# Half group 15 with both key tiles in parts, border terms summed on TensorE, and the 3x3 mask on VectorE, in an attention and local-attention kernel

## The chip, the cores and the metric

One core of one Trainium2 chip runs the whole program. The metric is the device time of one execution in microseconds (us). It is 3201.46 us before the change, the median of three runs (3201.24 to 3201.75).

## The reference

The input is `x`, 4 images of 64x64 pixels with 256 channels, in float32. Two layers follow each other.

```python
# layer 0: attention of every pixel of an image on all 4096 pixels of the image
q, k, v = x @ Wq + bq, x @ Wk + bk, x @ Wv + bv          # 32, 32 and 256 channels
attn = softmax(einsum('bnd,bmd->bnm', q, k))
x = gamma * einsum('bnm,bmc->bnc', attn, v) + x
# layer 1: three 3x3 depthwise filters per channel, a two-layer perceptron, a 3x3 local attention
hid = gelu(w_up1 @ conv3x3(x) + b_up1)                    # 768 -> 512 channels
h = x + w_up2 @ hid + b_up2
q, k, v = split(h @ w_qkv.T + b_qkv)                      # zero-padded at the image's border
out = h + sum over 9 neighbours of softmax(q . k / 16) * v
```

## The kernel before

**Blocks.** The 4 images are 32 blocks (`slot`, 0 to 31) of 512 pixels, 8 blocks an image, and all engines' queues are written out by hand in one order. In a block the 512 queries meet the image's 4096 keys in 16 half groups of two key tiles of 128 keys each. Half group n is worked on at point n of the block (n = 2G + half). At a point TensorE makes the scores `e` of the half group two ahead (L418), then the point's jobs of layer 1, then the products `acc` of half group n (L481). ScalarE makes `p = exp(e)` (L423). VectorE's work for half group n+1 (`add_up`, `low_and_gap`) stands at the end of point n, and after it come some steps of the 3x3 filters (`perc`, L687 and L693): `share` gives their number at each point: 2, 6, 8, 4, 7, 2, 7, 4, 6, 4, 3, 1, and none at points 12 to 15.

**Whole or in parts.** A key tile is multiplied either whole, in float32 (`acc<-p,v`, one product for each of two halves of the channels), or in parts: p is split into a rounded high part (`ph` or `oh`, ScalarE), a low part (`pl` or `ol`, L446 or L510) and a gap (`pg` or `og`, L447 or L520), which make three products for each half of the channels in the quicker fp32r format. Half groups 2, 4, ..., 14 have both tiles in parts by one operation on 1024 columns. In odd half groups one tile (the second) is in parts, by operations on 512 columns. In those of `BOTH_IN_PARTS` the first is too. This holds in the 25 "full" blocks (3 to 6, 8 to 14, 16 to 22, 24 to 30). The first tile's four pieces (values loaded by SyncE, high, low, gap) lie in the one buffer `hid`, which the perceptron also uses; those of the second lie in four buffers `vs`. Both show as `vo`, `oh`, `ol`, `og` in the trace. The values' parts are written to HBM once for each image by `project_v`.

**Layer 1, three to five blocks behind.** `border_terms` runs at the end of `update` (point 7): for the two side columns (8 pixels each), and in the first and last block of an image also for a row of 2 x 32 pixels, it weights the two halves of `h`'s channels with `wc` and adds them into `edge`; `border` (point 14) sums `edge` over the partitions by a product with ones (`c<-edge,ones`, L1004) and takes the exponential into `pad`. `local_values` (points 10 and 0) makes two tiles of local values with a bias. `scores` (points 11 and 12, one half of the columns each) makes the local scores `s`, their exponential `lp` (ScalarE, L1081) and the mask by `near` (GpSimd, L1086, in blocks before 30). `local_sum` (after the second mask) adds pieces of `lp` into `lsum` on GpSimd (L1109). GpSimd's queue also issues the transfers `sent<-p` (`send`, L498 and L500), by which the DMA sums up the weights.

**The end of a block.** After half group 15, VectorE adds the weights up (`den`, L513 to L529), transposes `den` and the `lsum` of an older block (L547), reduces each (`parts`, L548), and reads out the accumulators (`evacuate`, L567), all ahead of the next block's first perceptron sum (`hid<-hid_bc`, L807). At point 0 of the next block TensorE makes `hid_a`, `hid_bc`, the local values, and then `dps<-parts,fold` (L576, in `finish`), ahead of the next half group 0. `hid_a` and the local values take one of the two banks called `m`, and `hid_bc` and `dps` take the other by turns, so that `dps` has to wait until L807 has read `hid_bc`. In the second of the lines below the banks' order is fixed.

```python
            return {0: 0, NBLK - 1: RB - 1}.get(s % NBLK)          # edge_row: which blocks have a border row
            return bank("m", name) if turns[-1] == "m" else turns[-1](name)   # job_bank
            ps = bank("m", f"dps_{s}")[:, :n]                       # finish
```

Of the kernel before, what the change touches and what calls it, by code (L numbers as in the profile page):

```python
# [9 lines left out]
F32 = mybir.dt.float32  # L10
F32R = mybir.dt.float32r
AF = mybir.ActivationFunctionType
ALU = mybir.AluOpType
AX = mybir.AxisListType
PSUM = bass.MemoryType.PSUM

P = 128
B, H, W, C = 4, 64, 64, 256
N = H * W
CQK = C // 8  # L20
CH = C // P
HP, WP = H + 2, W + 2
NB = 512
RB = NB // W
# [18 lines left out]
NSLOT = B * NBLK  # L43
# [7 lines left out]
BELOW = 1.0 - 2.0**-13  # L51
IN_PARTS = (2, 4, 6, 8, 10, 12, 14)
ONE_IN_PARTS = (1, 3, 5, 7, 9, 11, 13, 15)
BOTH_IN_PARTS = (11, 13)
BY_DMA = (3, 5, 7, 9, 11, 13)
BY_DMA_IF_FULL = tuple(range(14))

# [5 lines left out]
def attention_then_perception_kernel(  # L63
# [19 lines left out]
    nc = tc.nc  # L83
# [8 lines left out]
    ones = const.tile([P, P], F32, tag="ones", name="ones")  # L92
# [8 lines left out]
    def unshifted():  # L101
        fctx = ExitStack()
        pool = fctx.enter_context(tc.tile_pool(name="fast", bufs=1))
# [4 lines left out]
        def tile_of(shape, tag, name, bufs=1):  # L108
            return pool.tile(shape, F32, tag=tag, name=name, bufs=bufs)
# [84 lines left out]
        def watch(values):  # L194

            n = values.free_size()
            for i in range(0, n, P):
                at = watched[:, : min(P, n - i)]
                nc.gpsimd.tensor_tensor(at, at, values[:, i : min(n, i + P)], ALU.add)
# [22 lines left out]
        def full(s):  # L222
            return in_two_sums(s) and s > 1 and s % NBLK < NBLK - 1
# [4 lines left out]
        def alone(s, n):  # L228

            return [i for i, ns in enumerate((BOTH_IN_PARTS, ONE_IN_PARTS)) if full(s) and n in ns]  # L230

# [110 lines left out]
        def project_v(s, pair, tag="m"):  # L342
# [10 lines left out]
            n = 2 * (s % NBLK) + pair  # L353
            split, one, both = (n in ns for ns in (IN_PARTS, ONE_IN_PARTS, BOTH_IN_PARTS))
            h = packed_h[:, s, bass.ts(pair, 2 * C)].rearrange("p (t c) -> p t c", c=C)
# [54 lines left out]
        parts_, inverses, turneds, evacuated = {}, {}, {}, {}  # L410
# [120 lines left out]
        def squares(t):  # L531
            return t.rearrange("p (j r) -> p j r", r=SQ)
# [6 lines left out]
        def partial_sums(s):  # L539


            a = shared(s)
            parts_[s] = tile_of([P, 2, NJ], "parts", f"parts_{s}")
            turneds[s] = tile_of([P, CH, NB], "xc", f"turned_{s}", 2)
            todo = [sums[s][:, 0, :]] + ([] if a is None else [lsums.pop(a)])
            for i, t in enumerate(todo):
                nc.vector.transpose(turneds[s][:, i, :], t)  # L547
                nc.vector.tensor_reduce(  # L548
                    parts_[s][:, i, :], squares(turneds[s][:, i, :]), axis=AX.X, op=ALU.add
                )  # L550
            watch(parts_[s][:, : len(todo), :].rearrange("p i j -> p (i j)"))

        def on_all(values, turned, out, copy=nc.vector.tensor_copy):

# [82 lines left out]
        def late_tile(name):  # L637

            if not thirds:
                t = perc_tile(name).rearrange("p s n -> p (s n)")  # L640
                thirds[:] = [t[:, i * NB : (i + 1) * NB] for i in range(3)]
            return thirds.pop(0)
# [237 lines left out]
        guides, lvs, near_ws, late, results, totals = [], {}, {}, {}, {}, {}  # L880
        wg = pool.tile([P, CH, C], F32, tag="wg", name="wg")
        small = pool.tile([P, 2 * CH + 1], F32, tag="small", name="small")
        bg, wc, bc = small[:, :CH], small[:, CH : 2 * CH], small[0:1, 2 * CH :]
# [82 lines left out]
        def edge_row(s):  # L966
            return {0: 0, NBLK - 1: RB - 1}.get(s % NBLK)

        edge = pool.tile([P, 2 * RB + W], F32, tag="edge", name="edge")

        def border_parts(s):

# [15 lines left out]
        def border_terms(s):  # L988


            for to, of in border_parts(s):
                nc.scalar.mul(edge[:, to], of(0), wc[:, 0:1])
                nc.vector.scalar_tensor_tensor(
                    edge[:, to], of(1), wc[:, 1:2], edge[:, to], ALU.mult, ALU.add
                )

        def border(s):


            ps = job_bank(f"c_{s}")  # L1000
            row = edge_row(s)
            n_side = 2 * RB
            n = border_parts(s)[-1][0].stop
            nc.tensor.matmul(ps[0:1, :n], lhsT=ones[:, 0:1], rhs=edge[:, :n], start=True, stop=True)  # L1004
            one = pad[0:1, :]
            nc.scalar.activation(one[:, :n], ps[0:1, :n], AF.Exp, bias=bc, scale=-(C**-0.5))
            nc.gpsimd.tensor_scalar(one[:, :n], one[:, :n], 3.0, None, ALU.mult)
            if row is not None:

                ends = one[:, n_side : n : W - 1]  # L1010
                nc.gpsimd.tensor_scalar(ends, ends, 2.0 / 3.0, None, ALU.mult)
# [4 lines left out]
        def local_values(s, t):  # L1016
            ps = job_bank(f"lv_{s}_{t}")
            for half in range(2):
                for kin in range(CH):
                    nc.tensor.matmul(  # L1020
                        ps[:, half * C : (half + 1) * C],
                        lhsT=keys_of(s, t, half, kin), rhs=wlv[:, kin, :],
                        start=(kin == 0), stop=(kin == CH - 1),
                    )
            for half in range(2):
                if s < NSLOT - 2:
                    lvs[s, t, half] = tile_of([P, C], "lv", f"lv_{s}_{t}_{half}", 8)
                else:
                    if not half:
                        late[s, t] = late_tile(f"lv_{s}_{t}")  # L1030
                    lvs[s, t, half] = late[s, t][:, half * C : (half + 1) * C]
                lv = lvs[s, t, half]
                nc.vector.tensor_tensor(lv, ps[:, half * C : (half + 1) * C], blv, ALU.add)
                if s >= NSLOT - 1:

                    square = tile_of([P, 2, NB], "den", f"lv_{s}_{t}_{half}_2")[:, 0, :C]
                    nc.gpsimd.tensor_tensor(square, lv, lv, ALU.mult)
                    watch(square)

        def pieces(s):  # L1040

# [9 lines left out]
        def scores(s, half):  # L1051


            g = s % NBLK
            ps = job_bank(f"s_{s}_{half}")

            tiles, rows, top = (2, QR, 0) if s < NSLOT else (1, UP, RB)
            n = tiles * rows * QW
            for t in range(tiles):
                for kin in range(CH):  # L1060
                    nc.tensor.matmul(  # L1061
                        ps[:, t * QR * QW : t * QR * QW + rows * QW].rearrange(
                            "p (h w) -> p h w", w=QW
                        ),
                        lhsT=keys_of(s, t, half, kin),
                        rhs=guides[0][:, kin, top + t * KR : top + t * KR + rows, columns(half)],
                        start=(kin == 0), stop=(kin == CH - 1),
                    )
            if s < NSLOT - 2:
                p = tile_of([P, 2 * QR * QW], f"lp{half}", f"lp_{s}_{half}", 2)  # L1070
            else:

                if s < NSLOT:
                    late[s] = late_tile(f"lp_{s}_{half}")
                elif not half:
                    late[s] = tile_of([P, NB], "lsum", f"lp_{s}")
                p = late[s][:, : 2 * QR * QW]
                if s == NSLOT:
                    p = late[s][:, half * C : half * C + QR * QW]
            near_ws[s, half] = p.rearrange("p (t h w) -> p t h w", h=QR, w=QW)  # L1080
            nc.scalar.activation(p[:, :n], ps[:, :n], AF.Exp, scale=C**-0.5)  # L1081
            pv = p[:, :n].rearrange("p (t n) -> p t n", t=tiles)
            mask = near[:, half, :rows, :].rearrange("p h w -> p (h w)")
            mask = mask.unsqueeze(1).to_broadcast([P, tiles, rows * QW])
            if s < NSLOT - 2:
                nc.gpsimd.tensor_tensor(pv, pv, mask, ALU.mult)  # L1086
            else:
                nc.vector.scalar_tensor_tensor(
                    pv, pv, 1.0, mask, ALU.mult, ALU.mult, accum_out=seen()
                )  # L1090

            if g == 0:
                nc.gpsimd.memset(p[P // 2 :, : UP * QW], 0.0)
                if s < NSLOT:
                    nc.gpsimd.memset(p[: P // 2, UP * QW : QR * QW], 0.0)
            if DIRECT <= s < NSLOT - 2:

                watch(p[:, :n])
# [115 lines left out]
        for slot in range(NSLOT):  # L1214
# [3 lines left out]
            k, a = slot - LAG_HID, slot - LAG_ATT  # L1218
# [48 lines left out]
            for point in range(points):  # L1267
                G, half = divmod(point, 2)
# [38 lines left out]
                if slot < NSLOT - 1:  # L1307
                    to = sum(share[: point + 1])
                else:
                    to = min(n_steps, -(-(point + 1) * n_steps // (points - 2)))  # L1310
                    if point < 3:
                        to = min(to, n_mixed // MULT)
# [3 lines left out]
                if slot == 0 and point == 1:  # L1316
                    wb = const.tile([P, CH, MULT, TAPS + 1], F32, tag="wb", name="wb")
                    nc.gpsimd.dma_start(out=wb[:, :, :, :TAPS], in_=w_perc)
                    bias = loaded(b_perc, "bperc", queue=nc.gpsimd)
# [20 lines left out]
                if slot == 1 and point == NG:  # L1340
# [7 lines left out]
                    blv = loaded(b_lv.partition_broadcast(P), "blv", [P, C], queue=nc.gpsimd)  # L1348
# [425 lines left out]
    with tc.manual_schedule():  # L1774
        wv, gam, wperc, bperc, wup1, bup1, wup2, bup2, blqk, blv = unshifted()
# [50 lines left out]
```

## Time and profile before

| | |
|---|---|
| median of three runs | 3201.46 us |
| the profiled execution | 3203.15 us |
| its span (first to last instruction) | 3201.4 us |
| TensorE busy | 3179.4 us (99%) |
| VectorE busy | 2903.6 us (91%) |
| ScalarE busy | 1550.8 us (48%) |
| GpSimd busy | 759.6 us (24%) |
| moved by DMA | 683.26 MB |

In the views, PE is TensorE (PEld its weight load), DVE is VectorE, ACT is ScalarE, POOL is GpSimd and SP is SyncE; a q behind the name means that engine's queue, which issues transfers. A float32 product counts as two instructions on PE. A line of the timeline gives the start in us from the span's start, the duration in us, engine, line of the code, operation, output<-inputs, shapes and count; in brackets stand the engine's idle time before it and what ended it. Matmuls overlap, and the end of one is modelled, so that lengths on PE are best read from start to start.

### The profile page before, as it was taken

The page shows a single profiled execution, that of the slowest core. Times are in us where ns is not written, and L with a number is a line of the kernel's source. Part 1 is how long each engine was busy: PE and PEld are TensorE (multiplying, and loading weights), DVE is VectorE, ACT ScalarE, POOL GpSimd, SP SyncE. Part 2 cuts the span into 40 slices and gives each one's busy share as a digit, 9 for nine tenths or more (in the row PEclk, how much of TensorE's full clock was granted, in tenths as well). Part 3 has the DMA queues.
Part 4 walks back from the last instruction along what each step waited for, and adds up shares of the span by engine and source line. Part 5 has one row for each costly group of instructions (what it writes and reads, how often), then busy time and mean ns, then how long its engine had stood idle before and what let it go on. Part 6 is the DMA issues. An engine that isn't in the chain of part 4 may idle for free.

```text
span 3201.4 us, 39239 instructions
## 1 busy us (share of the span) xinstructions
PE 3179.4 (99%) x12486; PEld 2261.7 (71%) x12486; DVE 2903.6 (91%) x4428; ACT 1550.8 (48%) x2068; POOL 759.6 (24%) x1055
## 2 busy tenths in 40 slices
PE   9999999999999999999999999999999999999998
PEld 5557777766777777776777777777677777777655
DVE  5778999998999999998999999998899999999894
ACT  4435555445545555544555545554555555455331
POOL 3201122212222221222122232211221222222121
PEclk9999999999999999999999999999999999999999
DMA  7768888777888888877878888886788888888100
GB/s 259 229 170 218 227 226 224 220 230 229 227 227 243 243 218 229 221 208 247 234 219 232 225 240 234 238 221 197 269 238 221 224 228 227 235 237 220 50 25 28
DMA packets 315588, 683.26 MB, mean 213 GB/s; under 512 B 100384, under 2 KB 101424, under 8 KB 315248
## 3 DMA queue, kind: packets, MB, share of 16 engines
q1 hardware_dynamic: 243008, 435.69, 42.6%
q0 software_dynamic: 64688, 231.54, 31.7%
q10 hardware_dynamic: 7680, 13.44, 1.1%
q8 instruction: 104, 1.70, 0.2%
q14 instruction: 108, 0.88, 0.1%
HBM read 412.46 MB, written 80.61 MB: 154 GB/s over the span
## 4 chain that ended last, share of the span: by engine, by line
PE 94%; DVE 3%; DMA 1%; issue 0%; POOL 0%; ACT 0%; SPq 0%; ACTq 0%; DVEq 0%; POOLq 0%
PE acc L481 46%; PE e L418 7%; PE dx L857 7%; PE hid_de L800 5%; PE hid_gf L800 5%; PE hid_bc L800 5%; PE lv L1020 3%; PE g L953 3%; PE lo L1154 3%; PE v L347 3%; PE s L1061 2%; PE hid_a L800 2%; DVE perc L687 1%; PE qk L272 1%; PE hid L832 1%; DMA vo<-packed_o 0%
## 5 line engine op out<-in xcount | busy, mean ns | idle before, releaser
L687 DVE SCALAR_TENSOR_TENSOR perc<-xp,wb,perc 128x526 f32<-128x526 f32 (+1 forms) x1356 | 937.7, 757 | 0.4
L423 ACT ACTIVATE p<-e 128x1024 f32<-128x1024 f32 x512 | 524.9, 1025 | 485.9 <-PE e L418 409.4
L481 PE MATMUL acc<-p,v 128*128 128x512 f32 x1472 | 678.9, 596 | 0.2 <-ACT v L363 0.2
L500 POOL DMA_DIRECT2D sent<-p x304 | 258.0, 855 | 1353.6 <-ACT p L423 823.0
L481 PEld LDWEIGHTS acc<-p,v 128*128 128x128 f32 x1472 | 275.1, 190 | 267.9 <-issue 257.6
L418 PE MATMUL e<-qa,ka 128*128 128x512 f32 x1024 | 357.1, 430 | 5.3 <-ACT p L423 1.5
L428 ACT ACTIVATE ph<-p 128x1024 fp32r<-128x1024 f32 x203 | 215.1, 1060 | 198.4 <-PE acc L481 134.7
L510 DVE TENSOR_TENSOR pl<-p,ph 128x1024 fp32r<-128x1024 f32 x203 | 256.1, 1262 | 16.8 <-ACT ph L428 16.8
L481 PE MATMUL acc<-ph,v 128*128 128x512 f32 x812 | 264.3, 447 | 0.2
L520 DVE SCALAR_TENSOR_TENSOR pg<-pl,ph 128x1024 fp32r<-128x1024 f32 x203 | 253.3, 1248 | 11.9 <-DVE pl L510 0.5
L418 PEld LDWEIGHTS e<-qa,ka 128*128 128x128 f32 x1024 | 190.9, 188 | 86.0 <-issue 39.9
L437 ACT ACTIVATE oh<-p 128x512 fp32r<-128x512 f32 x200 | 126.4, 632 | 248.4 <-PE acc L481 83.2
L857 PE MATMUL dx<-hid,wup 128*128 128x512 f32 x512 | 229.8, 592 | 0.0
L481 PE MATMUL acc<-pl,vf 128*128 128x512 f32 x812 | 223.3, 397 | 0.0
L481 PE MATMUL acc<-pg,vf 128*128 128x512 f32 x812 | 219.1, 391 | 2.0 <-DVE pg L520 2.0
L481 PEld LDWEIGHTS acc<-ph,v 128*128 128x128 f32 x812 | 148.2, 189 | 51.9 <-issue 26.8
L481 PE MATMUL acc<-oh,v 128*128 128x512 f32 x400 | 184.8, 543 | 0.0
L481 PEld LDWEIGHTS acc<-pg,vf 128*128 128x128 f32 x812 | 152.3, 188 | 39.1 <-DVE pg L520 3.3
L481 PEld LDWEIGHTS acc<-pl,vf 128*128 128x128 f32 x812 | 152.7, 188 | 37.1
L823 ACT ACTIVATE hid<-hid,bup 128x512 f32<-128x512 f32 x120 | 80.3, 716 | 199.1 <-DVE hid L807 199.1
L693 DVE TENSOR_TENSOR perc<-perc 128x262 f32<-128x262 f32 x360 | 170.8, 488 | 6.3
L857 PEld LDWEIGHTS dx<-hid,wup 128*128 128x128 f32 x512 | 96.7, 189 | 98.5 <-issue 93.4
(231 smaller groups left out, 5476.1 us busy)
## 6 DMA issues: line engine op xcount, KB each, us to landing
sent<-p POOLq DMA_DIRECT2D x356, 512.0 KB, 6.5
vf<-packed_f SPq DMA_DIRECT2D x203, 512.0 KB, 5.7
v<-packed_h SPq DMA_DIRECT2D x200, 512.0 KB, 4.7
ka<-packed SPq DMA_DIRECT2D x1016, 64.0 KB, 3.3
vo<-packed_o SPq DMA_DIRECT2D x250, 256.0 KB, 3.9
xp<-in_x SPq DMA_DIRECT2D x30, 528.0 KB, 6.9
packed_f<-vlg POOLq DMA_DIRECT2D x28, 512.0 KB, 4.3
xc<-in_x SPq DMA_DIRECT2D x56, 256.0 KB, 4.3
```

What stands on the lines that cost most here:

```text
L418: nc.tensor.matmul(e[:, i, :], lhsT=keys[s, G][:, bass.ts(2 * half + i, P)].bitcast(F32R), rhs=queries[s].bitcast(F32R), start=True, stop= ...
L423: nc.scalar.activation(p, e, AF.Exp)
L428: nc.scalar.activation(high.bitcast(F32R), weights[s, G, half], AF.Identity, scale=BELOW)
L437: nc.scalar.activation(high.bitcast(F32R), p, AF.Identity, scale=BELOW)
L481: nc.tensor.matmul(accs[s][to + c], lhsT=w[:, bass.ts(c, P)].bitcast(kind), rhs=x.bitcast(kind), start=to not in started[s], stop=last,)
L500: nc.gpsimd.dma_start(out=sent[s, even], in_=p, accum_op=ALU.add)
L510: nc.vector.tensor_tensor(low.bitcast(F32R), p, high, ALU.subtract)
L520: nc.vector.scalar_tensor_tensor(gap.bitcast(F32R), low, -SPLIT, high, ALU.mult, ALU.add)
L687: nc.vector.scalar_tensor_tensor(acc, win, wt, acc, ALU.mult, ALU.add)
L693: nc.vector.tensor_tensor(t[:, to, :], t[:, a, :], t[:, b, :], op)
L800: nc.tensor.matmul(ps[:, n * C : (n + 1) * C], lhsT=w(j), rhs=rows_of(mixes[s, j][:, kind, :]), start=(j == 0), stop=(j == MULT - 1),)
L857: nc.tensor.matmul(ps, lhsT=wup2[:, d, bass.ts(c, P)], rhs=hids[s][:, d, :], start=(d == 0), stop=(d == NHC - 1),)
```

## The change

Five edits stand in the diff. Half group 15 joins `BOTH_IN_PARTS`: in full blocks its first tile is now in parts as well, in the buffer `hid`. The border terms are weighted on ScalarE alone, for both halves of the channels, and TensorE adds the halves in two accumulating products. The two local value tiles get their bias in one operation of 512 columns instead of two of 256 (and so do the squares of the last block). The two reductions of the partial sums become one. The mask is multiplied on VectorE instead of GpSimd, at the same place of the program.

```diff
-BOTH_IN_PARTS = (11, 13)
+BOTH_IN_PARTS = (11, 13, 15)
...
             for i, t in enumerate(todo):
                 nc.vector.transpose(turneds[s][:, i, :], t)
-                nc.vector.tensor_reduce(
-                    parts_[s][:, i, :], squares(turneds[s][:, i, :]), axis=AX.X, op=ALU.add
-                )
-            watch(parts_[s][:, : len(todo), :].rearrange("p i j -> p (i j)"))
+            parts = parts_[s][:, : len(todo), :].rearrange("p i j -> p (i j)")
+            turned = turneds[s][:, : len(todo), :].rearrange("p i n -> p (i n)")
+            nc.vector.tensor_reduce(parts, squares(turned), axis=AX.X, op=ALU.add)
+            watch(parts)
...
-        edge = pool.tile([P, 2 * RB + W], F32, tag="edge", name="edge")
+        edge = pool.tile([P, CH, 2 * RB + W], F32, tag="edge", name="edge")
...
             for to, of in border_parts(s):
-                nc.scalar.mul(edge[:, to], of(0), wc[:, 0:1])
-                nc.vector.scalar_tensor_tensor(
-                    edge[:, to], of(1), wc[:, 1:2], edge[:, to], ALU.mult, ALU.add
-                )
+                for c in range(CH):
+                    nc.scalar.mul(edge[:, c, to], of(c), wc[:, c : c + 1])
...
-            nc.tensor.matmul(ps[0:1, :n], lhsT=ones[:, 0:1], rhs=edge[:, :n], start=True, stop=True)
+            for c in range(CH):
+                nc.tensor.matmul(
+                    ps[0:1, :n], lhsT=ones[:, 0:1], rhs=edge[:, c, :n],
+                    start=(c == 0), stop=(c == CH - 1),
+                )
...
+            if s < NSLOT - 2:
+                lv = tile_of([P, 2, C], "lv", f"lv_{s}_{t}", 4)
+            else:
+                lv = late_tile(f"lv_{s}_{t}").rearrange("p (a c) -> p a c", a=2)
             for half in range(2):
...
-                nc.vector.tensor_tensor(lv, ps[:, half * C : (half + 1) * C], blv, ALU.add)
...
+                lvs[s, t, half] = lv[:, half]
+            bias = blv.unsqueeze(1).to_broadcast([P, 2, C])
+            nc.vector.tensor_tensor(lv, ps.rearrange("p (a c) -> p a c", a=2), bias, ALU.add)
...
             if s < NSLOT - 2:
-                nc.gpsimd.tensor_tensor(pv, pv, mask, ALU.mult)
+                nc.vector.tensor_tensor(pv, pv, mask, ALU.mult)
```

More of the change, by code (lines that the diff above doesn't have):

```diff
@@ L1024, in local_values @@
                     )
+            if s < NSLOT - 2:
+                lv = tile_of([P, 2, C], "lv", f"lv_{s}_{t}", 4)
+            else:
+                lv = late_tile(f"lv_{s}_{t}").rearrange("p (a c) -> p a c", a=2)
             for half in range(2):
[L1026 to L1032, printed above, removed]
-                nc.vector.tensor_tensor(lv, ps[:, half * C : (half + 1) * C], blv, ALU.add)
[L1034 to L1038, printed above, removed]
+                lvs[s, t, half] = lv[:, half]
+            bias = blv.unsqueeze(1).to_broadcast([P, 2, C])
+            nc.vector.tensor_tensor(lv, ps.rearrange("p (a c) -> p a c", a=2), bias, ALU.add)
+            if s >= NSLOT - 1:
+                square = tile_of([P, 2, NB], "den", f"lv_{s}_{t}_2")[:, 0, :]
+                nc.gpsimd.tensor_tensor(square.rearrange("p (a c) -> p a c", a=2), lv, lv, ALU.mult)
+                watch(square)
         def pieces(s):
```

## The prediction

> **What bounds the kernel now.** I read the page first: the busy shares, the slices and the chain that ended last.
>
> ```profile
> PE 3179.4 (99%) x12486; PEld 2261.7 (71%) x12486; DVE 2903.6 (91%) x4428; ACT 1550.8 (48%) x2068; POOL 759.6 (24%) x1055
> ...
> DVE  5778999998999999998999999998899999999894
> ...
> PE 94%; DVE 3%; DMA 1%; issue 0%; POOL 0%; ACT 0%; SPq 0%; ACTq 0%; DVEq 0%; POOLq 0%
> ```
>
> TensorE is never short of work from the second slice on, and the chain lies on it for 94% of the span: a product saved there is worth its full length, as long as nobody else gets late. VectorE is the one that may: in a full block (92.7 us between two `dps`, by the windows view) it is busy for 88.9 us. So I took block 17 in the timeline, first TensorE at points 13, 14 and 15.
>
> ```profile
> 1696.91 0.61 PE L418 MATMUL e<-qa,ka 128*128 128x512 f32 x2
> 1697.37 0.62 PE L481 MATMUL acc<-vo,v 128*128 128x512 f32 x2
> ...
> 1700.09 0.61 PE L418 MATMUL e<-qa,ka 128*128 128x512 f32 x2
> 1700.63 0.20 PE L1004 MATMUL c<-edge,ones 128*1 128x16 f32 x2
> ...
> 1703.65 0.62 PE L418 MATMUL e<-qa,ka 128*128 128x512 f32 x2
> 1704.10 1.88 PE L481 MATMUL acc<-p,v 128*128 128x512 f32 x4
> 1705.41 1.03 PE L481 MATMUL acc<-oh,v 128*128 128x512 f32 x2
> ```
>
> Point 13 (both tiles in parts) lasts from 1696.91 to 1700.09, 3.18 us. Point 15 (one tile whole) lasts from 1703.65 to 1707.21, where the next `e` starts: 3.56 us. Next, the end of the block.
>
> ```profile
> 1709.15 0.69 DVE L548 TENSOR_REDUCE parts<-turned 128x16 f32<-128x512 f32 x1
> 1709.75 1.28 DVE L567 TENSOR_TENSOR o<-acc,o 128x512 f32<-128x512 f32 x2
> ...
> 1711.81 0.69 DVE L807 TENSOR_TENSOR hid<-hid_bc,hid 128x512 f32<-128x512 f32 x1 [0.79 <-ACT perc L683]
> ...
> 1713.28 0.30 PE L576 MATMUL dps<-parts,fold 128*128 128x32 f32 x2
> ```
>
> `dps` on TensorE takes the bank that L807 has read. Before L807, VectorE has had no pause since point 4 (1651.2): whatever it is given more in that stretch comes out here. There are 0.79 us of idle time before L807, and from its end (1712.50) to `dps` 0.78 us: a reserve of 1.57 us. Last, the masks.
>
> ```profile
> 1690.38 1.00 POOL L1086 TENSOR_TENSOR lp<-lp,near 128x396 f32<-128x396 f32 x1 [4.74 <-ACT lp L1081]
> 1690.48 1.20 DVE L693 TENSOR_TENSOR perc<-perc 128x262 f32<-128x262 f32 x1
> ...
> 1694.33 0.50 ACT L1081 ACTIVATE lp<-s 128x396 f32<-128x396 f32 x1 [0.32 <-PE s L1061]
> ```
>
> An L693 takes 0.43 us elsewhere; beside GpSimd's mask it takes 1.20. The second mask (1694.92) stretches an L447 from 0.69 to 1.34.
>
> **What the Trainium skill says.** "SBUF — State Buffer", section "SBUF: two separate sides": VectorE operations with two SBUF inputs and GpSimd operations that read SBUF exclude each other, the loser waits for a whole instruction. The trace agrees: 0.77 + 0.65 us lost on VectorE for two masks. "VectorE: DVE Perf Modes", section "The perf-mode tier table": a float32 operation on two tensors stays at the single rate. The trace agrees, 0.42 us for 256 columns and 0.69 for 512 (L1033, L446), so that 396 columns are about 0.55.
>
> **The change part by part**, for a full block of the usual kind (21 of the 25).
>
> *TensorE.* Point 15 becomes like point 13: 3.56 - 3.18 = 0.38 us less, on the path. For 25 blocks that is -9.5 us. `border` makes one product more in each of 32 blocks. Point 14, which has the same twelve products and an `e` as point 13, lasts 3.56 us, so the whole `c` costs 0.38 with both changes of number format. A second product behind the first pays no change of format. Ends: 0.03 (the two records of one `c` start that close together: 0.20 busy for two of 0.177) and 0.38; I take 0.06 in 24 blocks and 0.15 in the 8 with a row of 80 columns: +2.6 us in all, 1 to 12.
>
> *VectorE.* Added: a low part and a gap for the first tile, 1.32 us (the pair at point 11 runs from 1687.02 to 1688.34), and two masks of 0.55, 1.10 (ends 0.45 and 0.70 each, by the shorter and longer rows). Removed: two `edge` sums, 0.34 (1670.89 to 1671.23); one of two reductions' start, 0.06; one of two biases' start, 0.05. Sum +1.97 occupied. Against it, GpSimd's two masks no longer hold it up: 1.4 us. Ends for this: 0 (`local_sum` moves into the gap and does the same) and 1.4. I take 1.4, since the lsum additions run either way. Net +0.57.
>
> *The new wait.* The mask stands in VectorE's queue and has to wait for `lp`. The first finds it ready (1690.30 against about 1690.5). For the second, VectorE arrives near 1693.8 (earlier by the edges and by the first mask's gone hold-up) and `lp` ends at 1694.83: about 1.05 us idle, with `vo`, `ol` and `og` of half group 13 queued behind, which TensorE needs from 1697.82 to 1699.63; they are ready by 1698.7. About 0.5 us of hold-ups by `local_sum` fall into that gap. So +1.1 us reach L807.
>
> *The boundary.* TensorE comes 0.32 us earlier (0.38 - 0.06), so 1.57 - 0.32 = 1.25 us of reserve stand against 1.1: it holds, by 0.15. In blocks 8, 16 and 24, the first full ones of their images, and in block 4, the reserve is smaller (after block 8, L807 ends at 838.72 and `dps` starts at 839.05, no idle before). There VectorE is late enough not to wait for the second mask, and +0.57 makes `dps` about 0.3 later than now, in place of 0.32 earlier.
>
> *Others.* ScalarE gets one rounding (L437, 0.63 us) and two edge products (0.30 each, four in border blocks) a block; it is busy for 48 of 92.7 us, and pauses 1.29 us ahead of `oh` at point 14. The edge products wait for the second half of `h` as the VectorE sums did; behind them stand only `perc` starts and roundings. SyncE issues one more load of 256 KB (0.34 us) at point 14, when `hid` is freed by half group 13 (its gap product starts at 1698.5), ahead of the `vo` issue at 1699.41 and the keys at 1699.79. Loads of this line land in 3.9 us (2.5 to 9.8), and the values are needed at 1704.55; cover 1.2 us. If it goes, each us costs up to 25. GpSimd loses two masks, so that `sent<-p` of half group 13 is issued 1.9 us sooner; nothing waits for it. Storing the new parts happens four times, in blocks where VectorE is 85% busy: nothing. After block 31, the two masks of block 29 sit on VectorE's own chain (3094 to 3107): +1.1, but its hold-ups there (1.39 for 0.69, 1.43 for 0.74) go: nothing, ±1.
>
> **Sum.** -9.5 + 2.6 + 4 x (0.3 + 0.38) = -4.2 us. Against the profiled execution (3203.15 us; span 3201.4) that gives 3199.0. That execution is 1.7 us above the median of the runs shown, so against the median, 3201.46, it is 3197.3 us. A measurement of this kernel can tell about 0.2% (6.4 us) from no change, and 4.2 us lies within it.
>
> **The rivals.** *The gain stays whole.* The boundary absorbs everything, also in blocks 4, 8, 16 and 24, and the 0.58 us of waiting for `pg` at point 14 of blocks 8 and 24 goes, since no GpSimd mask holds VectorE up: -9.5 + 2.6 - 1 = -7.9, 3193.6; with the cheapest `c`, 3192. For it: the estimate above has a reserve in 21 blocks; against it: 0.15 us is little.
>
> *VectorE sets the block's length.* If the relief from GpSimd's masks does not come (`local_sum` starts up to 4 us earlier, beside half groups 12 to 14), L807 is late by up to 1.97 + 0.5 in place of 1.1. The delay decides from 1.25 + 0.32 = 1.57 us on. At 2.1 us, `dps` comes 0.53 later than now in 25 blocks, +13 us, with the borders' 1 left outside them 3215 us; at 2.5 it is 3224. For it: no pause of VectorE since point 4; against it: both stretched operations lie exactly beside masks.
>
> *The late load.* The first tile's values land after 1704.55. One us late in all blocks eats the gain and gives 3218; one of three blocks leaves 3205. Against it: half group 15's present load, at the same time, comes in less than 3.5 us.
>
> **How the numbers follow.** The likeliest case, a gain partly eaten at the block's end, has 0.48 and spans 3195 to 3205; the whole gain 0.36; the two slower rivals 0.16 together. The range reaches from 3191.5 (whole gain with the cheapest borders) to 3208 (first part of the slower cases). Faster 0.36, same 0.48, slower 0.16.
>
> **What would show it.** Right: `acc<-p,v` loses 100 records (25 blocks, two channel halves, two records each), point 15 lasts 3.18 us, point 14 3.6; VectorE's busy share stays near 91% (its records contain the hold-ups: +36 for parts, +33 masks, -18 edges, -8 biases, -35 hold-ups, in us) and would be 92% if they stay; it is idle ahead of the second mask until `lp` ends; TensorE waits at `dps` in blocks 4, 8, 16 and 24 only. Wrong: idle time of TensorE ahead of `dps` or of `acc<-ol,vo` in all full blocks, or point 14 longer than 3.8 us.

## The result, and the profile after

The change makes the kernel slower: 3208.81 us (median of 12 runs) against 3202.73 us for the kernel before on the same chip (12 runs), a ratio of 1.0021, 95% interval 1.0012 to 1.0030. The profiled execution of the kernel after took 3207.5 us, with a span of 3205.7 us; that is 4.3 us more than the span before, and the median moved by 6.1 us. I forecast a gain of 4.2 us, so about 10 us (8.5 between the two profiled executions) are to be explained.

First the page of the kernel after: busy shares, VectorE's slices, and the chain that ended last, by engine and by line.

```profile
PE 3173.1 (99%) x12600; PEld 2271.2 (71%) x12600; DVE 2900.9 (90%) x4366; ACT 1579.9 (49%) x2173; POOL 653.5 (20%) x992
...
DVE  4878999988999999988999999998899999999894
...
PE 90%; DMA 4%; DVE 3%; issue 1%; ACT 1%; SPq 1%; POOL 0%; ACTq 0%; DVEq 0%; POOLq 0%
PE acc L481 44%; PE e L418 7%; PE dx L857 7%; PE hid_gf L800 5%; PE hid_de L800 5%; PE hid_bc L800 4%; PE lv L1022 3%; PE g L953 3%; PE lo L1155 3%; PE v L347 2%; PE hid_a L800 2%; PE s L1062 2%; DMA vo<-packed_o 2%; DVE perc L687 1%; PE qk L272 1%
```

TensorE's busy time fell by 6.3 us, as the products saved would have it, and yet the span grew. The chain says where to look: its share on TensorE fell from 94% to 90%, that of transfers rose from 1% to 4%, and half of that stands under one name, `vo<-packed_o`, the loads of values for half groups with single tiles in parts. VectorE is no fuller than before. Next the waits of TensorE (us in total, times, the longest one).

```profile
PE acc L481 <- DMA vo<-packed_o: 5.2, 10, 1.1
PE qk L272 <- DMA xc<-in_x: 2.8, 1, 2.8
PE dps L576 <- DVE hid L807: 2.7, 3, 1.0
...
PE lv L1022 <- ACT hid L813: 1.3, 2, 1.0
```

In the kernel before, the first of these lines reads

```profile
PE acc L481 <- DMA vo<-packed_o: 0.4, 2, 0.2
```

The third does not show there at all, and the last stands at 0.2. (The second is one wait in the start, where these executions differ by some us and give them back by block 4.) To put the waits into their places I read the starts of all `e` in TensorE's timeline: from one half group's `e` to the next is a point. Summed over the 24 full blocks from 4 to 30, in us:

| | before | after | difference |
|---|---|---|---|
| point 13 | 77.28 | 85.24 | +7.96 |
| point 14 | 88.67 | 88.96 | +0.29 |
| point 15 | 85.55 | 76.20 | -9.35 |
| point 0 | 226.25 | 232.24 | +5.99 |
| all 16 points | 2227.92 | 2232.45 | +4.53 |

No other point moves by more than 0.4. (Each sum is from one execution, and a point that does the same work in two kernels can differ by up to 2 us between them: point 11 stands at 110.89 after and at 108.80 in experiment 3.) So point 15 gave what it was forecast to give, point 13 took most of it back, and point 0 the rest and more. Here are block 17's points 13 to 15 in the timeline of TensorE after, where nothing is late:

```profile
1699.76 0.62 PE L418 MATMUL e<-qa,ka 128*128 128x512 f32 x2
...
1702.94 0.61 PE L418 MATMUL e<-qa,ka 128*128 128x512 f32 x2
1703.48 0.25 PE L1003 MATMUL c<-edge,ones 128*1 128x16 f32 x4
...
1706.54 0.62 PE L418 MATMUL e<-qa,ka 128*128 128x512 f32 x2
...
1709.72 0.62 PE L418 MATMUL e<-qa,ka 128*128 128x512 f32 x2
```

Point 15 lasts 3.18 us in place of 3.56, point 14 with its second border product 3.60. The end of the same block, in VectorE's timeline:

```profile
1697.71 0.97 DVE L1087 TENSOR_TENSOR lp<-lp,near 128x396 f32<-128x396 f32 x1 [0.68 <-ACT lp L1082]
...
1712.31 1.22 DVE L550 TENSOR_REDUCE parts<-turned 128x32 f32<-128x1024 f32 x1
1713.44 1.28 DVE L567 TENSOR_TENSOR o<-acc,o 128x512 f32<-128x512 f32 x2
1714.64 0.68 DVE L807 TENSOR_TENSOR hid<-hid_bc,hid 128x512 f32<-128x512 f32 x1
```

VectorE does wait for the second mask's `lp`, and has no idle time left ahead of L807; `dps` starts at 1715.79, 0.47 us behind L807's end, and is not held. In an ordinary block the reserve of the boundary holds.

Now a block in which point 13 is late, block 21, whose point 13 starts at 2069.70. TensorE:

```profile
2069.70 0.62 PE L418 MATMUL e<-qa,ka 128*128 128x512 f32 x2
2070.15 0.61 PE L481 MATMUL acc<-vo,v 128*128 128x512 f32 x2
2071.83 1.17 PE L481 MATMUL acc<-vo 128*128 128x512 f32 x4 [1.06 <-DMA vo<-packed_o]
```

And the two queues that had a part in it, in the kernel after: GpSimd's, which issues the transfer of half group 13's weights, and SyncE's, which issues the loads of the values of the same half group.

```profile
2062.43 0.86 POOL L500 DMA_DIRECT2D sent<-p  x1 [4.12 <-ACT p L423]
```

```profile
2063.88 1.74 SPq L335 DMA_DIRECT2D vo<-packed_o  x2
```

The same two in block 21 of the kernel before (it runs 2.0 us ahead here):

```profile
2061.06 1.01 POOL L1086 TENSOR_TENSOR lp<-lp,near 128x396 f32<-128x396 f32 x1 [4.74 <-ACT lp L1081]
2062.02 0.87 POOL L500 DMA_DIRECT2D sent<-p  x1
```

```profile
2061.89 0.81 SPq L335 DMA_DIRECT2D vo<-packed_o  x2
```

Before, the mask stood ahead of the transfer in GpSimd's queue, and the transfer was issued just behind the loads. Without the mask it is issued when its weights are ready, 1.4 us ahead of the loads. That it is 512 KB against their 2 x 256 KB made me suspect the transfer.

### The profile page after: what moved, and what is told of

Read it like the earlier page. It is cut to its first block, busy times and chain, and to the rows that moved or that the text cites. A ratio compares the mean times of both kernels' runs of the same rounds, so it can differ in the third digit from the quotient of the medians.

```text
span 3205.7 us, 39521 instructions
## 1 busy us (share of the span) xinstructions
PE 3173.1 (99%) x12600; PEld 2271.2 (71%) x12600; DVE 2900.9 (90%) x4366; ACT 1579.9 (49%) x2173; POOL 653.5 (20%) x992
## 4 chain that ended last, share of the span: by engine, by line
PE 90%; DMA 4%; DVE 3%; issue 1%; ACT 1%; SPq 1%; POOL 0%; ACTq 0%; DVEq 0%; POOLq 0%
PE acc L481 44%; PE e L418 7%; PE dx L857 7%; PE hid_gf L800 5%; PE hid_de L800 5%; PE hid_bc L800 4%; PE lv L1022 3%; PE g L953 3%; PE lo L1155 3%; PE v L347 2%; PE hid_a L800 2%; PE s L1062 2%; DMA vo<-packed_o 2%; DVE perc L687 1%; PE qk L272 1%
## 5 line engine op out<-in xcount | busy, mean ns | idle before, releaser
L481 PE MATMUL acc<-p,v 128*128 128x512 f32 x1372 | 630.2, 595 | 0.2 <-ACT v L363 0.2
L481 PEld LDWEIGHTS acc<-p,v 128*128 128x128 f32 x1372 | 255.6, 190 | 252.6 <-issue 244.0
L510 DVE TENSOR_TENSOR pl<-p,ph 128x1024 fp32r<-128x1024 f32 x203 | 249.7, 1230 | 16.6 <-ACT ph L428 16.6
L481 PE MATMUL acc<-oh,v 128*128 128x512 f32 x400 | 174.5, 517 | 0.0
L693 DVE TENSOR_TENSOR perc<-perc 128x262 f32<-128x262 f32 x360 | 156.7, 449 | 6.3
```

Source lines behind the costliest of these rows:

```text
L481: nc.tensor.matmul(accs[s][to + c], lhsT=w[:, bass.ts(c, P)].bitcast(kind), rhs=x.bitcast(kind), start=to not in started[s], stop=last,)
L510: nc.vector.tensor_tensor(low.bitcast(F32R), p, high, ALU.subtract)
L693: nc.vector.tensor_tensor(t[:, to, :], t[:, a, :], t[:, b, :], op)
```

## The experiments

**Theory A**: the mask's move lets `sent<-p` of half group 13 start ahead of the two loads of half group 13, and these come late. **Rivals**: the loads come late because the kernel after loads 6.4 MB more, for half group 15 (theory B); VectorE has too much to do, whoever multiplies the mask, and sets the end of the block (theory C). From experiment 5 on, **theory D** is about point 0: VectorE's work for half group 15 makes `dps` late, and the larger split of the next image's values does harm in blocks 8, 16 and 24. Each run was timed against the kernel before on the same chip.

**1. The mask back on GpSimd**, all else as in the kernel after.

```diff
-                nc.vector.tensor_tensor(pv, pv, mask, ALU.mult)
+                nc.gpsimd.tensor_tensor(pv, pv, mask, ALU.mult)
```

> The changed kernel with one edit undone: the mask is back on GpSimd. Theory A (with the mask gone from GpSimd's queue, the transfer sent<-p of half group 13 starts 1.6 us sooner and delays the loads vo of half group 13, so that TensorE waits at point 13): these loads land in about 4.5 us again, and over the 24 full blocks 4 to 30 point 13 lasts 77 us in sum as in the kernel before, point 15 still 76; point 0 lasts 227 to 232 us; the time is 4 to 8 us below the kernel before, 3195 to 3199. Theory B (the loads vo of half group 13 are late because the change loads 6.4 MB more): point 13 stays at 85 us and the time at 3208. Theory C (VectorE is overloaded, whoever does the mask): point 0 lasts over 235 us, time 3205 to 3210.

Measured: 3202.77 us against 3204.11, ratio 0.9997 (0.9989 to 1.0005). Point 13 is back at 78.21 us. The mask's move is what makes point 13 long; the extra bytes of half group 15, which are still loaded, are not (theory B). But point 0, at 234.37, stays as long as after, and the gain of 4 to 8 us that I expected did not come: the kernel is level with the one before.

**2. The mask alone**: the kernel before, with only the mask moved to VectorE.

```diff
-                nc.gpsimd.tensor_tensor(pv, pv, mask, ALU.mult)
+                nc.vector.tensor_tensor(pv, pv, mask, ALU.mult)
```

> The kernel before with the mask moved to VectorE and nothing else. Theory A: the loads vo of half group 13 land in about 6.9 us, point 13 lasts about 85 us in sum over the 24 full blocks against 77, point 15 stays at 85.5; time 5 to 10 us above the kernel before. Theory B: loads in 4.5 us, point 13 at 77, time within 2 us of the kernel before. Theory C: point 13 as before, point 0 over 229 us.

Measured: 3210.20 us, ratio 1.0019 (1.0011 to 1.0027). Point 13 is 85.03, point 0 225.86. This edit alone makes the kernel as slow as the whole change does.

**3. The transfer held back**: the kernel after, with an operation of one column on GpSimd that reads the first mask's product, so that the transfer behind it in the queue waits for VectorE's mask.

```diff
+        hold = pool.tile([P, 1], F32, tag="hold", name="hold")
...
                 nc.vector.tensor_tensor(pv, pv, mask, ALU.mult)
+                if half == 0:
+                    nc.gpsimd.tensor_copy(hold, p[:, :1])
```

> The changed kernel, in which GpSimd copies one column of the first masked tile into a spare tile, at the place where its mask had been: sent<-p of half group 13 cannot be issued before VectorE's first mask. Theory A: the issue is back at about 8.5 us after point 10's start (6.9 in the changed kernel), the loads land in 4.5 us, point 13 lasts 77 to 79 us; point 0 grows to 232 to 236, since VectorE no longer gains time at point 13; time 3 to 8 us below the changed kernel. Theory B and theory C: no difference from the changed kernel.

Measured: 3199.14 us, ratio 0.9984 (0.9977 to 0.9990): faster than the kernel before, with the mask still on VectorE, and more below the kernel after than the 3 to 8 us that I expected. Block 17 in GpSimd's timeline:

```profile
1688.93 1.11 POOL L1090 COPY hold<-lp 128x1 f32<-128x1 f32 x1 [5.42 <-DVE lp L1088]
1689.99 0.85 POOL L500 DMA_DIRECT2D sent<-p  x1
```

SyncE issued the loads at 1689.07; the transfer now comes 0.92 us behind them, and point 13 is 77.02.

**4. Without half group 15**: the kernel after, with `BOTH_IN_PARTS` as before.

```diff
-BOTH_IN_PARTS = (11, 13, 15)
+BOTH_IN_PARTS = (11, 13)
```

> The changed kernel without half group 15 in parts: the mask on VectorE, the edges by TensorE, and the merged operations stay. Theory A: point 13 lasts about 85 us, point 15 85.5, point 0 as in the kernel before or less (226): 6 to 10 us above the kernel before. Theory B: point 13 back at 77, time of the kernel before plus the edges' 2 us. Theory C: point 0 at 226, point 13 at 77 to 79, time of the kernel before plus 2.

Measured: 3210.77 us, ratio 1.0023 (1.0016 to 1.0030). Point 15 is back at 85.46, point 13 stays at 86.08, and point 0 falls to 226.00, the value before. So half group 15 has no part in point 13, and it is half group 15 that lengthens point 0.

**5. Half group 15 alone**: the kernel before, with only `BOTH_IN_PARTS = (11, 13, 15)`.

> The kernel before with half group 15 in parts and nothing else. Theory A (the send of half group 13 is what delays its loads): point 13 stays at 77 to 79 us over the 24 full blocks, point 15 at 76. Theory D (VectorE's work for half group 15 makes dps late at point 0 of blocks 9, 17 and 25, and the larger projection of the next image's values at point 0 of 8, 16 and 24): point 0 lasts 233 to 237 us against 226; without the edges' relief of 0.34 us also some of the other blocks wait. Time 2 to 6 us below the kernel before, worse or equal to the kernel with the mask alone undone (ratio 0.9997). If the border terms' two products cost what the prediction said, point 14 is 1.2 us shorter here than in the changed kernel.

Measured: 3212.35 us, ratio 1.0027 (1.0015 to 1.0038). The expectation missed, by sign. Point 15 does fall, to 76.34, but point 0 rises to 242.88. The waits of TensorE's weight load show by what:

```profile
PEld dps L576 <- DVE hid L807: 13.4, 17, 2.1
```

Seventeen times `dps` waits for L807, as late as 2.1 us. The parts of half group 15 put 1.32 us on VectorE ahead of the end of each block (my estimate from the pair at point 11), and without the relief that the other edits give that is more than the reserve allows. In experiment 3 the same line reads 5.4 us in 9 places. Experiment 1 says which edits give the relief: it has the edges, the bias and the reduction as in the kernel after and the mask on GpSimd, and its point 0 is 234.37. So these three edits together are worth 8.5 us at point 0, and the mask on VectorE, with the transfer held, another 1.4 at most (232.96 in experiment 3), which is within the spread of such sums. Which of the three does most was not tried.

**6. One step of the 3x3 filters sooner**: the kernel of experiment 3, with one `perc` step moved from point 10 to point 1, away from the end of the block.

```diff
-            share = [2, 6, 8, 4, 7, 2, 7, 4, 6, 4, 3, 1, 0, 0, 0, 0]
+            share = [2, 7, 8, 4, 7, 2, 7, 4, 6, 4, 2, 1, 0, 0, 0, 0]
```

> The kernel with the send held, and one filter step of VectorE moved from point 10 to point 1, where VectorE has 0.3 to 0.4 us of idle time. Theory D: VectorE reaches the end of the block 0.4 to 0.6 us sooner, dps waits less: point 0 falls from 233 to about 229.5 us, the rest stays; 2 to 4 us below the kernel with the send held. Rival (TensorE waits at point 0 for something other than VectorE): point 0 stays at 233.

Measured: 3199.84 us, ratio 0.9990 (0.9983 to 0.9996), no gain over experiment 3: a miss. Point 0 falls by 0.85 us where I expected 3.5, and point 4 grows by 2.25 (113.84 to 116.09), where in this kernel `e` waits for `p`; the waits list has that at 3.4 us in 6 places against 1.5 in one. I did not look further into why `p` is late there.

**7. Half group 15's first tile whole in the first block of an image**: the kernel of experiment 3, in blocks 8, 16 and 24 with the tile as before.

```diff
-            return [i for i, ns in enumerate((BOTH_IN_PARTS, ONE_IN_PARTS)) if full(s) and n in ns]
+            first = () if n == 15 and s % NBLK == 0 else BOTH_IN_PARTS
+            return [i for i, ns in enumerate((first, ONE_IN_PARTS)) if full(s) and n in ns]
```

> The kernel with the send held, without half group 15 in parts in blocks 8, 16 and 24, in which VectorE also adds up half groups 0 and 1. Theory D: point 0 loses 1.0 to 1.2 us in blocks 9, 17 and 25, point 15 grows by 0.38 us in blocks 8, 16 and 24: 1.5 to 2.5 us below the kernel with the send held in the trace. Rival (the wait at blocks 9, 17, 25 is not from half group 15): 1.2 us above it.

Measured: 3196.43 us, ratio 0.9981 (0.9974 to 0.9987), the lowest of all kernels here, though its interval and that of experiment 3 overlap, so that a gain over experiment 3 is not shown by the times. The excess of point 0 over its usual 9.33 us goes from 0.56, 1.24 and 1.24 us to nothing in blocks 9, 17 and 25, the ones that follow those three; point 15 gives 1.1 us back. From the end of point 0 of blocks 8, 16 and 24 to the end of the next point 0, the three stretches are 2.8 us shorter in sum than in experiment 3. So in the first full block of an image, where VectorE also has to add two half groups more (0 and 1), the parts of half group 15 cost more than they bring. What stays is the excess in blocks 8, 16 and 24 themselves: 2.11, 1.30 and 1.93 us, against 0.50, 0.19 and 1.40 before.

**8. Experiments 6 and 7 together.**

> The two last edits together. Theory D: point 0 at about 227 to 228 us, 8 to 10 us below the kernel before (3194 to 3196 where that is at 3203), the lowest of all. Rival: as the kernel with the send held, 0.9984 of the kernel before.

Measured: 3198.33 us, ratio 0.9986 (0.9979 to 0.9993). I expected the lowest time of all; the step brings nothing here either.

**9. Only the transfer moved**: the kernel before, with `sent<-p` of half group 13 issued at point 11, ahead of the first mask, in place of point 12.

```diff
-                if by_dma(*at):
-                    send(*at)
+                for n in {12: (12, 13), 13: ()}.get(at[1], (at[1],)):
+                    if by_dma(at[0], n):
+                        send(at[0], n)
```

> The kernel before with one thing moved: in GpSimd's queue the transfer sent<-p of half group 13 is issued at point 11, ahead of the first mask, in place of point 12, behind it. No instruction is added or taken away, masks stay on GpSimd, half group 15 keeps one tile whole. Theory A (the loss of the change is this transfer meeting the two value loads of half group 13): issue near 7 us after point 10's start in place of 8.5, those loads land in 6 to 7 us in place of 4.5, the sum of the 24 point 13s rises from 77 to 83 to 86 us, and the time is 5 to 8 us above the kernel before (ratio 1.0015 to 1.0025). Rival (the mask on VectorE is what delays, through VectorE's or SBUF's use, and the sooner transfer only goes with it): point 13 stays near 77 and the time within 2 us of the kernel before.

Measured: 3215.82 us, ratio 1.0034 (1.0022 to 1.0047), by its median no smaller a loss than that of the whole change (the intervals overlap) and larger than the 5 to 8 us that I expected; point 13 is 88.26. From the list of transfers, `vo<-packed_o` with its count, size and median us from issue to landing over all points, first before, then here:

```profile
vo<-packed_o SPq DMA_DIRECT2D x250, 256.0 KB, 3.9
```

```profile
vo<-packed_o SPq DMA_DIRECT2D x250, 256.0 KB, 5.1
```

No instruction was added, no mask is on VectorE, no half group has more parts. The order of one transfer and two loads, alone, makes a loss of that size, so neither VectorE's mask nor the parts are needed for it.

**All of them side by side.** From the issues and landings of the transfers: by how much `sent<-p` is issued after the first load of half group 13, and when the values of the two tiles land after the start of point 13 (medians of 24 blocks, us).

| kernel | transfer after load | first lands | second lands | sum of point 13 |
|---|---|---|---|---|
| before | +0.13 | -1.78 | +0.07 | 77.28 |
| 1 mask on GpSimd | +0.08 | -1.64 | +0.17 | 78.21 |
| 3 transfer held | +0.93 | -1.77 | -1.04 | 77.02 |
| 7 held, 15 not in first blocks | +0.95 | -1.66 | -0.99 | 76.74 |
| after | -1.44 | +0.86 | +2.01 | 85.24 |
| 2 mask alone | -1.44 | +1.01 | +1.89 | 85.03 |
| 4 without 15 | -1.44 | +1.03 | +1.95 | 86.08 |
| 9 only the transfer sooner | -1.44 | +1.19 | +2.14 | 88.26 |

The loads are issued 5.70 us ahead of point 13 in all of them (medians again). Block by block, in the kernel after and in experiment 9, the first load alone accounts for the loss: wherever it lands later than 0.65 us after the start of point 13, the point is longer than 3.17 us by just that much, within 0.1 us (after, block 21: landing +2.00, excess 1.35; block 13: +1.86 and 1.21; block 29: +1.15 and 0.51). That is so in 15 of the 24 blocks after, and in 19 in experiment 9. The kernel after has its own control: in blocks 11, 19 and 27 the transfer is issued behind the first load (by 1.51, 0.40 and 0.40 us), that load lands 1.9 to 2.6 us ahead of point 13, and the point lasts 3.17 us. In the view of TensorE's weight loads some of these waits stand under VectorE's `ol` and `og`. There VectorE had long been done: in block 21 of experiment 9 `ol` ended at +0.40 and `og` at +1.19, while TensorE stood from +0.68 to +2.32 and the load landed at +2.18.

**10. The stores apart.** What lengthens point 0 of blocks 8, 16 and 24? There ScalarE and VectorE finish splitting the next image's values, a job of the block before, the last of its image. In the four kernels that don't split half group 15's first tile (before, experiments 2, 4 and 9) the three points exceed 9.33 us by 1.9 to 2.8 us in sum, in the kernels above that do by 4.2 to 8.4. Block 24's point 0 in the timeline of experiment 3, ScalarE and TensorE:

```profile
2301.13 0.60 ACT L389 ACTIVATE vh<-v 128x512 fp32r<-128x512 f32 x1 [0.37 <-DMA packed_h<-vh]
...
2301.78 1.56 PE L800 MATMUL hid_bc<-perc,wup 128*128 128x256 f32 x6 [1.23 <-ACT vh L389]
```

And in the kernel before:

```profile
2305.17 0.60 ACT L389 ACTIVATE vh<-v 128x512 fp32r<-128x512 f32 x1
...
2305.82 1.56 PE L800 MATMUL hid_bc<-perc,wup 128*128 128x256 f32 x6 [0.46 <-ACT vh L389]
```

`hid_bc` takes the bank that `vh` has read. `vh` of half group 14 now has to wait for a buffer until a store of half group 15's `vh` is through: half group 15 takes four of the four buffers `vs` where it took three. In blocks 8 and 16 `hid_bc` is not later than before, and the wait falls on the next in line for these buffers, `oh` of half group 1. Block 8's point 0 in the kernel after, ScalarE and TensorE:

```profile
741.76 0.63 ACT L437 ACTIVATE oh<-p 128x512 fp32r<-128x512 f32 x1 [1.34 <-DMA packed_o<-vl]
743.21 0.36 ACT L813 COPY hid<-hid_a 128x256 f32<-128x256 f32 x1
743.62 1.99 PE L1022 MATMUL lv<-wlv,h 128*128 128x256 f32 x8 [1.01 <-ACT hid L813]
```

And ScalarE in the kernel before, where `lv` does not wait:

```profile
741.79 0.63 ACT L437 ACTIVATE oh<-p 128x512 fp32r<-128x512 f32 x1 [0.43 <-DMA packed_h<-vh]
```

`oh` waits for the store of half group 15's low part `vl`, a piece that the kernel before does not make as a buffer of its own. Behind `oh` in ScalarE's queue stands the copy of `hid_a`, and the local values `lv` take that bank next. In block 16 `oh` waits 0.72 us and `lv` 0.33. These are the two waits of `lv` in the list at the beginning. So I gave half group 15's low part and gap another buffer, in the kernel of experiment 7.

```diff
                 low, gap = (fresh(f"v{x}_{s}_{pair}") for x in "lg")
...
+                if n == 15:
+                    lg = tile_of([P, 2, NB], "sent", f"vlg_{s}_{pair}")
+                    low, gap = (lg[:, i].rearrange("p (t c) -> p t c", c=C) for i in range(2))
```

> The kernel of e9_15_not_first with one thing more: where the values of half group 15 of the next image are split (last block of an image), low part and gap are made in the buffer `sent` in place of two of the four buffers `vs`, so that half group 14's split, next in line, need not wait for half group 15's stores to free a buffer. Theory (point 0 of blocks 8, 16 and 24 grew since ScalarE's vh L389, ahead of hid_bc and the local values, waits for a buffer that a store still reads): excess of these three point 0s over 9.33 us falls from 5.3 us to about 2.1, as in the kernel before, and the time falls by 2 to 3 us against e9_15_not_first. Rival (the wait only moves, to vlg L388, which takes `sent` next and waits for half group 15's low part and gap to be stored): excess stays at 5 us or above, time equal or up to 3 us longer.

Measured: 3218.60 us, ratio 1.0042 (1.0028 to 1.0055). The rival was right, though its bound of 3 us was not: half group 14's own low part and gap take `sent` next, and now they wait for half group 15's stores, far longer. ScalarE's timeline at point 0 of block 24, and the waits of TensorE in this kernel:

```profile
2326.20 0.59 ACT L393 COPY vlg<-v 128x512 f32<-128x512 f32 x1 [4.25 <-DMA packed_v<-vs]
```

```profile
PE hid_bc L805 <- ACT vh L394: 14.5, 3, 5.4
```

The three point 0s exceed 9.33 us by 22.9 us in place of 5.3 in experiment 7. (Of the stores that L393 may wait for, the trace names the one with the last event; its buffer is `sent`, which half group 15's parts hold.) The run shows that this place is ruled by buffers that stores still read. A version that frees it, with a fifth buffer `vs`, was not tried.

## Why the prediction was wrong

**The step that failed** is this one: "GpSimd loses two masks, so that `sent<-p` of half group 13 is issued 1.9 us sooner; nothing waits for it." The first half is right (1.57 us sooner, relative to the loads). The second looks only at the transfer itself: nothing waits for it, but the two loads issued after it now land 2.6 and 1.9 us later, and TensorE waits for the first of them. I asked who waits for the moved transfer, and not what is next to be issued after its new place. It costs 8.0 us at point 13. Taken away alone (experiment 3) it turns +0.21% into -0.16%; put in alone (experiment 9) it gives +0.34%.

**A second step failed**: "Storing the new parts happens four times, in blocks where VectorE is 85% busy: nothing." VectorE was the wrong place to look. The new low part and gap take one buffer more, and ScalarE waits for a buffer, at half group 14's split in block 24 and at `oh` in blocks 8 and 16; TensorE waits for ScalarE, at `hid_bc` and at `lv`: point 0 of blocks 8, 16 and 24 costs 2.1 us more in the kernel after (1.47, 0.79 and 1.92 in place of 0.50, 0.19 and 1.40 us above 9.33). That these waits come from the fourth buffer is read from the traces; experiment 4 shows only that half group 15 is the cause, and experiment 10 that buffers decide there.

**A term that was mis-sized**: the boundary of the first full blocks. I put `dps` 0.3 us later than now after blocks 4, 8, 16 and 24. Behind block 4 nothing shows. After 8, 16 and 24 point 0 lasts 9.33 + 1.17, 1.24 and 1.13 us, 3.3 us more than before in sum. Most of that is not lost time: TensorE comes to this boundary sooner, by 0.38 us at point 15 and in blocks 8 and 24 by another 0.9 at point 14, where a wait is gone (4.51 to 3.61 and 3.63), in block 16 by 0.7 at point 11, and then waits for VectorE. From the end of point 0 of these blocks to the end of the next one it took 93.57, 93.67 and 93.58 us before and takes 93.40, 93.75 and 93.40 after: 0.3 us less in sum, where I had 0.9 more. The mechanism is the one named (VectorE sets this boundary, `dps` waits for L807), as experiment 7 shows; but VectorE's stretch did not grow by the 0.57 us of the forecast. In block 8, L807 ends 89.99 us after the end of point 0, and 89.98 before.

**Right**: point 15, -9.35 us in 24 blocks (forecast -9.1); the second border product, 0.05 us on an undisturbed point 14, 3.56 to 3.61 (0.06), and 0.11 with a row of 80 columns, 3.68 to 3.79 (0.15), though no run shows that the change of number format is what makes the first one dear; `acc<-p,v`, down from 1472 to 1372 records; the wait of VectorE for the second mask (0.68 us in block 17; I had 1.05); and the reserve of the ordinary blocks, which holds.

**Off, without harm**: VectorE's busy time, forecast 8 us up, fell by 2.7. The 60 masks take 41 us where I had 33: 0.57 each while GpSimd rests, as forecast, but over 0.7 in 19 of them, each beside one of GpSimd's `lsum` sums. The operations that both kernels have are 54 us shorter, where I had 35 for the hold-ups. The rule that I took from the Trainium skill ("SBUF — State Buffer", section "SBUF: two separate sides") agrees with both: with GpSimd's masks gone, an L693 takes 449 ns on average in place of 488, a `pl<-p,ph` of 1024 columns 1230 in place of 1262.

**The rivals.** "VectorE sets the block's length" fell for this kernel, but is what happens with half group 15 alone (experiment 5). "The late load" had the right kind of mechanism and the wrong load: half group 15's new load lands in 2.7 us (median of 24 blocks), as fast as its single load did, and at the latest 1.6 us ahead of point 15; it was half group 13's that came late. I had looked for the new transfer's own delay, and not for what the moved one does to others. (Its 3218 us for a load late in all blocks adds 25 us to the whole gain; added to the sum of the prediction they make 3222.)

## What to carry to other kernels

An operation that stands in a queue ahead of a transfer is also a clock: taking it away starts the transfer sooner. List for each such transfer which loads are issued within its length after the new start, how long they take now, and how much time they have: here 5.70 + 0.65 us of cover stood against 3.9 us from issue to landing of the first load (-1.78 + 5.70), and with the transfer 1.57 us sooner the load took 6.6. Where an order among transfers happens to be good, fix it by a dependence (experiment 3's copy of one column), so that a change of an engine's work can't undo it; and where a change stores one more piece, count buffers, not busy shares.

## What the runs showed of the hardware that was not expected

A 512 KB transfer on GpSimd's queue, issued 1.44 us ahead of two 256 KB loads on SyncE's, delays the first of them by 2.6 us and the second by 1.9 (landing at +0.86 and +2.01 in place of -1.78 and +0.07). Issued 0.13 us behind the first load in place of 0.93 us, it leaves the first alone and costs the second 1.1 us. The transfer itself takes 7.5 us in the kernel before and 7.6 in the kernel after: here the loads alone pay, and more than the 1.6 us by which it was moved.

The packets in the traces fit this. Between issue and landing of the first load the 16 DMA engines are full in all four kernels looked at (packet times add up to 1.0 of their time); of GpSimd's queue, 204 KB start in that stretch in the kernel before, 528 KB in the kernel after, 92 KB with the transfer held and 536 KB in experiment 9 (medians of 24 blocks). How the engines divide themselves between the two queues was not measured.
